# Depthwise filters of a convolution layer on sixteen 32x32 parts of TensorE, with half a block moved there from VectorE and the steps reordered

## Chip, cores and metric

The kernel runs on one core of one Trainium2 chip. The metric is the time of one execution in device microseconds (us). It is given as the median of several runs; the profile comes from one further execution with the hardware profiler on.

## What is computed

The reference chains four convolution layers over a tensor x of 32 images, 96 channels and 56 x 56 pixels in fp32. Each layer adds its result to its input, and takes as input a group normalisation of x (32 groups of three channels). The change concerns layer 0 alone, an inverted bottleneck with squeeze and excite:

```
def _L0_conv_ref(x, w_exp, ..., w_dw, ..., w_se1, b_se1, w_se2, b_se2, w_proj, ...):
    identity = x                                        # x is already group-normalised
    h = jnp.einsum('nchw,oc->nohw', x, w_exp)           # 96 -> 576 channels
    h = jax.nn.silu(_bn(h, g1, b1, m1, v1))
    h = conv_general_dilated(h, w_dw, padding='SAME', feature_group_count=MID)   # 3x3 depthwise
    h = jax.nn.silu(_bn(h, g2, b2, m2, v2))
    s = h.mean(axis=(2, 3))
    s = jax.nn.silu(s @ w_se1.T + b_se1)                # squeeze, 576 -> 24
    s = jax.nn.sigmoid(s @ w_se2.T + b_se2)             # excite, 24 -> 576
    h = h * s[:, :, None, None]
    h = jnp.einsum('nchw,oc->nohw', h, w_proj)          # project, 576 -> 96
    return _bn(h, g3, b3, m3, v3) + identity
...
x = x + _L0_conv_ref(_gn(x), ...)
```

Layers 1 to 3 (a wavelet convolution, a quantised bottleneck and a 9 x 9 diffusion filter) follow in the same program and are not touched.

## The kernel before

Layer 0 works through the 32 images one by one. The 576 inner channels make four and a half blocks of 128 partitions. The last half block holds 64 channels and is computed twice, once in each half of the partitions, which makes five blocks. An image has four tiles of 14 rows (`NP` = 4); the columns of a tile are split by parity (`j`), so that one TensorE product has 392 columns.

The work on one image is cut into steps. Each step is a letter in a hand-written order string, `L0_ORDER`, followed by up to two digits for the block and the tile or tap:

- `s`, `u`, `m`, `q`, `v`, `w`, `b`, `n`: the group normalisation. `s` and `q` are full passes on ScalarE that sum the image and its squares (L267); `u` and `v` are tiny TensorE products over the groups (L272); `m`, `w`, `b` are small VectorE steps (L276 to L290), `w` with one on GpSimd; `n` writes the normalised image `xn` (L295). `r` scales the image in place for the residual (L301).
- `e` (block, tile): expand. TensorE multiplies `xn` by the expanding weights (L309), and ScalarE evicts the result with batch norm and SiLU into a padded image `hpad` (L313).
- Blocks 0, 1 and 2 have their 3 x 3 depthwise filter on VectorE: `f` is the first tap, on ScalarE (L321), the eight `t` are the others, one `scalar_tensor_tensor` over the whole block each (L326), and `z` is the second batch norm and SiLU in place on ScalarE (L332), which also accumulates the channel sums.
- Blocks 3 and 4 (called AB and C) have their filter on TensorE, `a` and `c`: for each of nine taps four products with 64 x 64 diagonal matrices on four quarters of the array (`quarters`, L349), into one PSUM buffer, evicted by `silu2` (L332). Two of the four swap the upper and the lower 64 channels, so that all four parts of the array are in use.
- `g0` to `g4`: the channel sums are added up (VectorE), the squeeze (TensorE L379, ScalarE L381), the excite (TensorE L386), the gates (VectorE L391 and L392, ScalarE L393) and the projecting weights times the gates, `wg` (VectorE L397).
- `p` (tile): project. For each parity five products add up in PSUM, three with `h2` of blocks 0 to 2 (L407), one with `hab` (L409), one with `hc` (L410). `d` adds the result to the image on VectorE (L415).
- `o`: channel statistics for the next layer's normalisation (VectorE L88, L89), then on SP's queue the store of the image to `y0` in six DMAs (L425), the load of image b + 3 into the buffer that image b leaves (`fetch`, L196; there are three such buffers), and some seven sets of copies, here called table copies, that lay out filter tables of later layers in DRAM (L520, L547).

`run_steps` walks the order string once per slot n; a step with `+` works on image n + 1, with `-` on image n - 1. TensorE, VectorE and ScalarE run their instructions in exactly this order (`manual_schedule`), each waiting only for data and buffers; a step issues to its engines in the place where it stands. SP's queue is in order as well. PSUM has three buffers `mm` of two banks for all the large products and two small ones `sm` for the tiny products. `hpad` has two padded images that blocks 0 to 2 take in turn, and one each for AB and C; `h2` has five full-size buffers.

Of the kernel before, what the change touches and what calls it, by code (L numbers as in the profile page):

```python
# [25 lines left out]
RT = 7  # L26
# [36 lines left out]
    e00 e01 e02 e03 z0- f0 a3- z2- c1- e10 e11 t01 t02 g0- e12 t03 e30 e40 g1- s+ e13 t04 g2- g3-  # L63
    e31 e32 t05 e33 g4- t06 t07 u+ f1 m+ t11 p0- p1- q+ t08 d0- v+ w+ p2- t12 e41 d1- p3- d2- t13
    t14 e20 e21 d3- o- b+ t15 e42 t16 e43 e22 e23 f2 a0 t17 t21 a1 n+ t22 t18 t23 t24 t25 t26 t27 r
    z1 t28 c0 a2
# [9 lines left out]
class Shared:  # L76


    def load(self, nc, w):
        for t, n in ((self.grp, "group"), (self.ident, "ident"), (self.bias1, "l1_bias")):  # L80
            nc.sync.dma_start(t, w[n])
# [76 lines left out]
def window(t, p, dy, dx, r0, rows):  # L158

    at = (r0 + 1 + dy) * PITCH + 1 + dx  # L160
    return t[:p, at : at + rows * PITCH].rearrange("p (r w) -> p r w", w=PITCH)[:, :, 0:W]
# [3 lines left out]
def layer0(ctx, tc, S, x, w, y0, norm1, tables, aside):  # L165
# [8 lines left out]

    nc = tc.nc
# [3 lines left out]
    psum = ctx.enter_context(tc.tile_pool(name="l0p", bufs=3, space=PSUM))  # L179
    psm = ctx.enter_context(tc.tile_pool(name="l0q", bufs=2, space=PSUM))  # L180
    DV, AB, CC = 3, 3, 4
    ND = NBLK + 1
    COL = (0, 1, 2, 3, 5)
    HALF = 64

    def load(name, shape):
        t = cp.tile(shape, F32, tag=name, name=name)
        nc.sync.dma_start(t, w[name])
        return t
# [12 lines left out]
    wdw = load("l0_wdw", [128, ND, 9])  # L202
    wse1 = load("l0_wse1", [128, ND, SEH])
    wse2 = load("l0_wse2", [SEH, ND * 128])
    bse1 = load("l0_bse1", [SEH, 1])
    wproj = load("l0_wproj", [128, ND + 1, C])
# [25 lines left out]
    eye2 = cp.tile([128, HALF], F32, tag="eye2", name="eye2")  # L232
    diag = cp.tile([128, 2, 9, HALF], F32, tag="diag", name="diag")
# [6 lines left out]
    nc.vector.tensor_tensor(eye2, S.ident[:, :HALF], S.ident[:, HALF:], ALU.add)  # L240
    for k in (AB, CC):
        for t in range(9):
            nc.vector.tensor_scalar(diag[:, k - AB, t, :], eye2, wdw[:, COL[k], t : t + 1], None, ALU.mult)
    late = ctx.enter_context(tc.tile_pool(name="l0l", bufs=1))
    h2s += [late.tile([128, H, W], F32, tag=f"h2{i}", name=f"h2{i}") for i in (2, 3)]
    hab = late.tile([128, NP, 2, NT], F32, tag="hab", name="hab")
    wg = late.tile([128, ND + 1, C], F32, tag="wg", name="wg")
    h2s.append(late.tile([128, H, W], F32, tag="h24", name="h24"))
    hc = late.tile([128, 2, 2, NT], F32, tag="hc", name="hc")
# [3 lines left out]
    def image(b):  # L253

        if b not in ims:
            ims[b] = {
                "b": b, "xt": xs.pop(b), "h2": [None] * DV, "ps": [None] * NP,
                "pad": [hpad[(DV * b + k) % 2] for k in range(DV)] + hpad[2:],
                "ss": sm.tile([128, ND], F32, tag="ss", name="ss"),
            }  # L260
        return ims[b]
# [8 lines left out]
    def group_sum(im, name):  # L270
        im["ps" + name] = psm.tile([C, 1], F32, tag="sm", name="pn")
        nc.tensor.matmul(im["ps" + name], S.grp, im[name], start=True, stop=True)  # L272
# [46 lines left out]
    def first_tap(im, k):  # L319
        im["h2"][k] = h2s[(DV * im["b"] + k) % len(h2s)]  # L320
        nc.scalar.activation(im["h2"][k], window(im["pad"][k], 128, -1, -1, 0, H), AF.Copy,  # L321
                             scale=wdw[:, k, 0:1])

    def tap(im, k, t):
        h2 = im["h2"][k]
        nc.vector.scalar_tensor_tensor(  # L326
            h2, window(im["pad"][k], 128, t // 3 - 1, t % 3 - 1, 0, H), wdw[:, k, t : t + 1],
            h2, ALU.mult, ALU.add,
        )

    def silu2(c, view, ps, accum):
        nc.scalar.activation(view, ps, AF.Silu, bias=bi[1][:, c : c + 1], scale=sc[1][:, c : c + 1],  # L332
                             accum_out=accum)
# [4 lines left out]
    def quarters(k, pad, tiles):  # L338


        ps = psum.tile([128, 2, 512], F32, tag="mm", name="psd")
        for t in range(9):
            for j in range(2):
                for r in range(2):
                    c = r ^ j
                    p = slice(r * HALF, (r + 1) * HALF)
                    at = (2 * tiles[r] * RT + t // 3) * PITCH + t % 3
                    v = pad[p, at : at + 2 * RT * PITCH].rearrange("p (r w) -> p r w", w=PITCH)
                    nc.tensor.matmul(  # L349
                        ps[c * HALF : (c + 1) * HALF, j, :NT].rearrange("p (r w) -> p r w", w=W2),  # L350
                        diag[p, k - AB, t, :], v[:, :, j:W:2], start=(t == 0), stop=(t == 8),
                    )
        return ps

    def depthwise_ab(im, i):
        if i == 0:
            im["hab"] = hab
            im["pab"] = sm.tile([128, 2, NP], F32, tag="pab", name="pab")
        ps = quarters(AB, im["pad"][AB], (i, i))
        for j in range(2):  # L360
            silu2(3 + j, im["hab"][:, i, j, :], ps[:, j, :NT], im["pab"][:, j, i : i + 1])

    def depthwise_c(im, i):

        if i == 0:
            im["hc"] = hc
            im["pc"] = sm.tile([128, 2], F32, tag="pc", name="pc")
        ps = quarters(CC, im["pad"][CC], (2 * i, 2 * i + 1))
        silu2(5, im["hc"][:, i], ps[:, :, :NT], im["pc"][:, i : i + 1])


    def totals(im):
        nc.vector.tensor_reduce(im["ss"][:, 3:5], im["pab"], AX.X, ALU.add)
        nc.vector.tensor_tensor(im["ss"][:, 5:6], im["pc"][:, 0:1], im["pc"][:, 1:2], ALU.add)

    def squeeze(im):
        ps = psm.tile([SEH, 1], F32, tag="sm", name="pse")
        for k in range(ND):
            nc.tensor.matmul(ps, wse1[:, k, :], im["ss"][:, k : k + 1], start=(k == 0), stop=(k == ND - 1))  # L379
        im["s1g"] = sm.tile([SEH, 1], F32, tag="s1g", name="s1g")  # L380
        nc.scalar.activation(im["s1g"], ps, AF.Silu, bias=bse1, scale=1.0 / HW)  # L381

    def excite(im):
        im["pg"] = psm.tile([128, ND], F32, tag="sm", name="pg")
        for k in range(ND):
            nc.tensor.matmul(im["pg"][:, k : k + 1], wse2[:, k * 128 : (k + 1) * 128], im["s1g"],  # L386
                             start=True, stop=True)

    def gates(im):
        gt = im["gate"] = sm.tile([128, ND + 1], F32, tag="gate", name="gate")  # L390
        nc.vector.tensor_tensor(gt[:, :ND], im["pg"], mid[:, 8, :], ALU.add)  # L391
        nc.vector.tensor_tensor(gt[:, ND:], im["pg"][:, ND - 1 : ND], mid[:, 8, ND - 1 : ND], ALU.add)  # L392
        nc.scalar.activation(gt, gt, AF.Sigmoid)  # L393

    def gated(im):
        im["wg"] = wg
        nc.vector.tensor_tensor(im["wg"], wproj, im["gate"].unsqueeze(2).to_broadcast([128, ND + 1, C]),  # L397
                                ALU.mult)

    def project(im, i):  # L400
        wg = im["wg"]
        rows = slice(2 * i * RT, 2 * (i + 1) * RT)
        ps = im["ps"][i] = psum.tile([128, 2, 512], F32, tag="mm", name="psj")
        for j in range(2):
            out = ps[:C, j, :NT]
            for k in range(DV):
                nc.tensor.matmul(out.rearrange("c (r w) -> c r w", w=W2), wg[:, k, :],  # L407
                                 im["h2"][k][:, rows, j::2], start=(k == 0), stop=False)
            nc.tensor.matmul(out, wg[:, 3 + j, :], im["hab"][:, i, j, :], start=False, stop=False)  # L409
            nc.tensor.matmul(out, wg[:, 5 + (i % 2 ^ j), :], im["hc"][:, i // 2, j, :], start=False, stop=True)  # L410
# [9 lines left out]
    def store(im):  # L420
# [16 lines left out]
        "e": expand, "f": first_tap, "t": tap, "z": end_block, "a": depthwise_ab, "c": depthwise_c,  # L437
# [840 lines left out]
def layouts(a):  # L1278
# [7 lines left out]
    def quartered(v):  # L1286


        v = blocks(v)
        ba = np.concatenate([v[64:, 3], v[:64, 3]])  # L1290
        cc = np.concatenate([v[:64, 4], v[:64, 4]])
        return np.concatenate([v[:, :4], ba[:, None], cc[:, None]], axis=1)
# [7 lines left out]

    def apart(v):

        v = np.concatenate([v, v[:, -1:]], axis=1)
        v[64:, -2] = 0.0
        v[:64, -1] = 0.0
        return v

    def columns(names, blocks):
# [11 lines left out]
        "l0_wdw": quartered(a[i0 + "w_dw"].reshape(MID, 9)),  # L1320
        "l0_wse1": quartered(a[i0 + "w_se1"].T),
        "l0_wse2": quartered(a[i0 + "w_se2"]).transpose(2, 1, 0).reshape(SEH, (NBLK + 1) * 128),
        "l0_bse1": a[i0 + "b_se1"].reshape(SEH, 1),
        "l0_wproj": apart(quartered(a[i0 + "w_proj"].T)),
# [9 lines left out]
        "l2_w2": quartered(a[i2 + "w2"].reshape(MID, 9))[:, [0, 1, 2, 3, 5]],  # L1334
# [34 lines left out]
```

## Time and profile before

| | us |
|---|---|
| median of 3 runs | 6412.01 |
| lowest and highest run | 6397.1, 6412.93 |
| the profiled execution's own time | 6501.16 |
| its span, first to last instruction | 6499.3 |
| layer 0's first image statistics (L88) in it | 182.9 |
| layer 0's last image statistics in it | 3340.9 |

All durations below come from the profiled execution. Engines are PE (TensorE matmul), PEld (its weight loads), DVE (VectorE), ACT (ScalarE), POOL (GpSimd) and SP (SyncE, which issues DMAs). A line of the costliest groups reads: source line, engine, operation, out<-in by the program's names, shapes, count | busy us in all, mean ns of one | idle time of the engine just before them and what ended it. A line of a timeline reads: start, duration, engine, line, operation, names, shape, count, and in brackets the idle time before it with its releaser. A line of waits reads: who waited <- for whom: us in all, times, longest. The end of a matmul in the trace is modelled, so starts are the better measure of TensorE's pace.

### The profile page before, as it was taken

How to read it: one execution, taken by the hardware profiler on the slowest of the kernel's cores; microseconds unless marked ns; L12 is line 12 of the kernel's file. 1: busy time of each engine (PE TensorE's matmuls, PEld its weight loads, DVE VectorE, ACT ScalarE, POOL GpSimd, SP SyncE). 2: the span in 40 equal slices, each digit the busy share in tenths (PEclk: the TensorE clock that was granted, in tenths of full speed). 3: DMA queues.
4: the chain of work that ended last, by engine and by line, in shares of the span. 5: the costliest groups of instructions: out<-in, count | busy, mean ns of one | idle time of the engine just before them, and what ended most of it. 6: DMA issues, size and time to landing. Idle time of an engine off the chain costs nothing.

```text
span 6499.3 us, 115397 instructions
## 1 busy us (share of the span) xinstructions
PE 6025.5 (93%) x49064; PEld 3599.1 (55%) x49064; DVE 5168.3 (80%) x5469; ACT 3953.6 (61%) x5268; POOL 234.1 (4%) x157
## 2 busy tenths in 40 slices
PE   6989989998998998989969999989999999999699
PEld 3444444444444444444535666667777777778344
DVE  8989979898998998989957766657777767676587
ACT  6556555655656565556635565557767766677355
POOL 4000000000000000000000000000000000000000
PEclk8999999999999999989979999999999999999899
DMA  2486475839539439474655776656869695953888
GB/s 80 29 41 50 41 43 41 46 44 40 47 41 41 43 47 42 39 41 39 17 60 143 141 155 150 143 36 45 48 42 50 44 49 41 51 38 31 166 253 248
DMA packets 1631554, 452.94 MB, mean 70 GB/s; under 512 B 1447406, under 2 KB 1625318, under 8 KB 1627582
## 3 DMA queue, kind: packets, MB, share of 16 engines
q1 hardware_dynamic: 1631038, 445.55, 65.7%
q8 instruction: 386, 6.32, 0.6%
q14 instruction: 130, 1.06, 0.1%
HBM read 284.44 MB, written 214.08 MB: 77 GB/s over the span
## 4 chain that ended last, share of the span: by engine, by line
PE 71%; ACT 9%; DMA 9%; SPq 6%; DVE 3%; issue 1%; POOL 1%; ACTq 0%; DVEq 0%
PE psd L349 14%; PE psd L1019 11%; PE ps L309 9%; PE psj L407 8%; PE pc L735 6%; PE ps L1000 5%; SPq L425 4%; DMA y<-xt 4%; PE pc L1175 3%; PE psj L1056 3%; PE psj L409 3%; PE psj L410 2%; ACT hi L972 2%; ACT a L990 2%; DVE h L326 2%; PE pc L719 2%
## 5 line engine op out<-in xcount | busy, mean ns | idle before, releaser
L326 DVE SCALAR_TENSOR_TENSOR h<-hpad,l_wdw,h 128x3136 f32<-128x3136 f32 x768 | 2659.6, 3480 | 28.7 <-ACT h L321 14.9
L349 PE MATMUL psd<-hpad,diag 64*64 64x392 f32 x13824 | 1239.6, 512 | 13.4 <-issue 13.4
L313 ACT ACTIVATE hpad<-ps,o,s 128x784 f32<-128x784 f32 x640 | 684.3, 1081 | 773.3 <-PE ps L309 771.3
L309 PE MATMUL ps<-xn,l_wexp 96*128 96x392 f32 x2560 | 931.6, 516 | 135.6 <-ACT hpad L313 129.1
L1019 PE MATMUL psd<-apad,diag 64*64 64x392 bf16 x20736 | 931.5, 332 | 110.4 <-ACT a L990 57.2
L349 PEld LDWEIGHTS psd<-hpad,diag 64*64 64x64 f32 x13824 | 547.5, 132 | 694.9 <-issue 656.8
L1019 PEld LDWEIGHTS <-diag 64*64 64x64 bf16 x20736 | 695.6, 107 | 342.3 <-issue 164.7
L309 PEld LDWEIGHTS ps<-xn,l_wexp 96*128 96x128 f32 x2560 | 493.4, 197 | 524.2 <-ACT hpad L313 135.3
L565 ACT COPY T<-raw 32x112 f32<-32x112 f32 (+2 forms) x1440 | 462.8, 384 | 308.1 <-DMA raw<-tdiff 223.3
L990 ACT ACTIVATE u<-ps,o,s 128x784 int16<-128x784 f32 x576 | 536.3, 1002 | 162.0 <-PE ps L1000 143.6
L990 ACT ACTIVATE a<-psd,o,s 128x784 int16<-128x784 f32 x448 | 423.7, 999 | 327.7 <-PE psd L1019 327.7
L407 PE MATMUL psj<-h,wg 128*96 128x392 f32 x1536 | 591.4, 520 | 27.9 <-ACT hpad L313 26.4
L1000 PE MATMUL ps<-hi,l_w1q 96*128 96x392 f32 x1280 | 462.4, 361 | 10.0 <-ACT hi L972 9.2
L1175 PE MATMUL pc<-x,T 128*112 128x416 f32 (+1 forms) x1152 | 415.2, 523 | 48.1 <-DMA raw<-tdiff 47.6
L735 PE MATMUL pc<-x,T 128*112 128x416 f32 (+1 forms) x1152 | 445.8, 523 | 0.0
L1000 PE MATMUL ps<-lo,l_w1q 96*128 96x392 f32 x1280 | 438.0, 342 | 0.0
L407 PEld LDWEIGHTS psj<-h,wg 128*96 128x96 f32 x1536 | 249.4, 166 | 289.3 <-issue 258.3
L1175 PEld LDWEIGHTS pc<-x,T 128*112 128x112 f32 x1152 | 204.7, 178 | 258.1 <-issue 240.7
L332 ACT ACTIVATE hab<-psd,o,s 128x392 f32<-128x392 f32 x256 | 170.6, 671 | 263.5 <-PE psd L349 263.5
L332 ACT ACTIVATE h<-h,o,s 128x3136 f32<-128x3136 f32 x96 | 287.9, 2999 | 19.7 <-DVE h L326 19.7
L321 ACT ACTIVATE h<-hpad,l_wdw 128x3136 f32<-128x3136 f32 x96 | 279.1, 2907 | 9.3 <-DMA twav<-zwav 8.3
L735 PEld LDWEIGHTS pc<-x,T 128*112 128x112 f32 x1152 | 190.9, 178 | 143.9 <-issue 143.9
(202 smaller groups left out, 6793.5 us busy)
## 6 DMA issues: line engine op xcount, KB each, us to landing
X<-y SPq DMA_DIRECT2D x192, 392.0 KB
xt<-in_x_dram SPq DMA_DIRECT2D x32, 1176.0 KB
y<-xt SPq DMA_DIRECT2D x192, 196.0 KB
y<-y SPq DMA_DIRECT2D x96, 392.0 KB
xt<-y SPq DMA_DIRECT2D x96, 392.0 KB
out_dram<-y SPq DMA_DIRECT2D x96, 392.0 KB
y<-xt SPq DMA_DIRECT2D x90, 392.0 KB
twav<-zwav SPq DMA_DIRECT2D x768, 36.8 KB
```

The costliest lines, as they stand in the source:

```text
L309: nc.tensor.matmul(ps[:, j, :NT], wexp[:, k * 128 : k * 128 + 128], im["xn"][:, j, rows, :].rearrange("c h w -> c (h w)"), start=True, sto ...
L313: nc.scalar.activation(window(im["pad"][k], 128, 0, 0, 2 * i * RT, 2 * RT).rearrange("p r (w j) -> p j r w", j=2), ps[:, :, :NT].rearrange ...
L326: nc.vector.scalar_tensor_tensor(h2, window(im["pad"][k], 128, t // 3 - 1, t % 3 - 1, 0, H), wdw[:, k, t : t + 1], h2, ALU.mult, ALU.add,)
L332: nc.scalar.activation(view, ps, AF.Silu, bias=bi[1][:, c : c + 1], scale=sc[1][:, c : c + 1], accum_out=accum)
L349: nc.tensor.matmul(ps[c * HALF : (c + 1) * HALF, j, :NT].rearrange("p (r w) -> p r w", w=W2), diag[p, k - AB, t, :], v[:, :, j:W:2], start ...
L407: nc.tensor.matmul(out.rearrange("c (r w) -> c r w", w=W2), wg[:, k, :], im["h2"][k][:, rows, j::2], start=(k == 0), stop=False)
L565: nc.scalar.copy(to.rearrange("x t (p s) -> x t p s", p=NPH), v[:, k])
L735: nc.tensor.matmul(ps[:PH, to], st["T"][j][:, h, k, :], st["x"][:, j, h, of], start=False, stop=(n == NK - 1))
L990: nc.scalar.activation(out, ps, AF.Identity, bias=o[:, c : c + 1], scale=s[:, c : c + 1])
L1000: nc.tensor.matmul(ps[:, j, :NT], w1[:, k * 128 : k * 128 + 128], im[part][:, r0 : r0 + RT, :].rearrange("c h w -> c (h w)"), start=(part ...
L1019: nc.tensor.matmul(ps[q, j, :NT].rearrange("p (r w) -> p r w", w=W), diag[p, k, t, :], v, start=(t == 0), stop=(t == 8))
L1175: nc.tensor.matmul(ps[:, :, to], st["T"][:, h, k, :], st["x"][:, h, :, of], start=(n == 0), stop=(n == NK - 1))
```

## The change

Layer 0's filters on TensorE now use sixteen 32 x 32 parts of the array. The new `parts` replaces `quarters`. It takes two PSUM buffers (four banks) at once. For every tap it issues sixteen products with 32 x 32 diagonal matrices: shift `s` picks the column parity and the tile and owns one bank, and row part `r` writes to partition quarter `(r + s) % 4`. The channels of a shift's output are thus turned by `s` quarters, and the weights that meet them later (batch norm, squeeze, excite, project) are laid out in as many turned copies. One call covers two tiles of a block; so `a` is two calls per image in place of four, and `c` is one in place of two.

Block 2 is split. Its upper two tiles stay on VectorE (`f2`, `t2x`, `z2` on 28 rows, buffer `h2c`); its lower two go to TensorE in a new step `x0` (output `hd`). The number of columns of sums, gates and projecting weights grows: `ND` from 6 to 12, the gated weights from 7 to 14 groups. The project step still makes five products per parity: for the lower two tiles, `hd` takes the place of block 2's `h2`.

PSUM is one pool of four two-bank buffers, from which the tiny products are served too. `h2` has three full buffers and one half. The order of the steps is new: image n + 1's first block is expanded at the end of a slot; `g0` and `g1` stand at the end of the slot, `g2-` to `g4-` open the next, `p` and `d` follow in its first half, `s+` comes after `p1-`, and `x0`, `a0`, `c0`, `a1` follow one another on TensorE.

The setting up of the layer changes with it (27 small diagonal products in place of 18, and other layouts of the weights, made before the launch). The core of the diff:

```diff
-L0_ORDER: e00 e01 e02 e03 z0- f0 a3- z2- c1- e10 e11 t01 t02 g0- e12 t03 e30 e40 g1- s+ e13 t04 g2- g3-
-    e31 e32 t05 e33 g4- t06 t07 u+ f1 m+ t11 p0- p1- q+ t08 d0- v+ w+ p2- t12 e41 d1- p3- d2- t13
-    t14 e20 e21 d3- o- b+ t15 e42 t16 e43 e22 e23 f2 a0 t17 t21 a1 n+ t22 t18 t23 t24 t25 t26 t27 r
-    z1 t28 c0 a2
+L0_ORDER: g2- g3- e40 t01 g4- e12 t02 t03 e30 t04 e41 e13 p0- d0- p1- s+ u+ t05 p2- m+ r t06 d1- t07 d2-
+    p3- q+ f1 t08 e42 d3- e31 e32 e33 e20 v+ e21 o- w+ t11 e22 e23 t12 b+ e43 f2 t13 t14 t21 t15 z0
+    x0 t16 a0 t22 t17 t18 n+ c0 t23 z1 t24 t25 t26 a1 t27 e00+ t28 z2 e01+ e02+ g0 e03+ g1 f0+ e10+
+    e11+
...
-    psum = ctx.enter_context(tc.tile_pool(name="l0p", bufs=3, space=PSUM))
-    psm = ctx.enter_context(tc.tile_pool(name="l0q", bufs=2, space=PSUM))
-    DV, AB, CC = 3, 3, 4
-    ND = NBLK + 1
-    COL = (0, 1, 2, 3, 5)
+    psum = ctx.enter_context(tc.tile_pool(name="l0p", bufs=4, space=PSUM))
+    DV, XX, AB, CC = 3, 2, 3, 4
+    COL = (0, 1, 2, 6, 10)
+    ND, NW = 12, 14
+    QU = 32
...
-    for k in (AB, CC):
+    for k in (XX, AB, CC):
         for t in range(9):
-            nc.vector.tensor_scalar(diag[:, k - AB, t, :], eye2, wdw[:, COL[k], t : t + 1], None, ALU.mult)
+            nc.vector.tensor_scalar(diag[:, k - XX, t, :], eye4, wdw[:, k, t : t + 1], None, ALU.mult)
...
+                "h2": [h2s[2 * b % 3], h2s[(2 * b + 1) % 3], h2c],
...
     def group_sum(im, name):
-        im["ps" + name] = psm.tile([C, 1], F32, tag="sm", name="pn")
+        im["ps" + name] = psum.tile([128, 2, 512], F32, tag="mm", name="pn")[:C, 0, :1]
...
-    def quarters(k, pad, tiles):
-        ps = psum.tile([128, 2, 512], F32, tag="mm", name="psd")
+    def parts(im, k, tile, out, accum, col):
+        ps = [psum.tile([128, 2, 512], F32, tag="mm", name="psd") for _ in range(2)]
         for t in range(9):
-            for j in range(2):
-                for r in range(2):
+            for s in range(4):
+                for r in range(4):
+                    p, q = (slice(x % 4 * QU, (x % 4 + 1) * QU) for x in (r, r + s))
+                    at = (2 * tile(r, s) * RT + t // 3) * PITCH + t % 3
+                    v = im["pad"][k][p, at : at + 2 * RT * PITCH].rearrange("p (r w) -> p r w", w=PITCH)
                     nc.tensor.matmul(
+                        ps[s // 2][q, s % 2, :NT].rearrange("p (r w) -> p r w", w=W2),
+                        diag[p, k - XX, t, :], v[:, :, s % 2 : W : 2], start=(t == 0), stop=(t == 8),
                     )
+        for s in range(4):
+            silu2(col(s), out[s], ps[s // 2][:, s % 2, :NT], accum(s))
+    def depthwise_ab(im, g):
+        parts(im, AB, lambda r, s: 2 * g + s // 2, [hab[:, 2 * g + s // 2, s % 2] for s in range(4)],
+              lambda s: im["pq"][:, g, s : s + 1], lambda s: COL[AB] + s)
+    def depthwise_c(im, _):
+        parts(im, CC, lambda r, s: 2 * (r // 2) + s // 2, [hc[:, s] for s in range(4)],
+              lambda s: im["pc"][:, s : s + 1], lambda s: COL[CC] + s % 2)
+    def depthwise_x(im, _):
+        parts(im, XX, lambda r, s: 2 + s // 2, [hd[:, s] for s in range(4)],
+              lambda s: im["ss"][:, XX + s : XX + s + 1] if s else im["px"], lambda s: XX + s)
...
     def project(im, i):
...
-            for k in range(DV):
+            s = 2 * (i % 2) + j
+            for k in range(DV if i < 2 else XX):
                 nc.tensor.matmul(out.rearrange("c (r w) -> c r w", w=W2), wg[:, k, :],
                                  im["h2"][k][:, rows, j::2], start=(k == 0), stop=False)
-            nc.tensor.matmul(out, wg[:, 3 + j, :], im["hab"][:, i, j, :], start=False, stop=False)
-            nc.tensor.matmul(out, wg[:, 5 + (i % 2 ^ j), :], im["hc"][:, i // 2, j, :], start=False, stop=True)
+            if i >= 2:
+                nc.tensor.matmul(out, wg[:, XX + s, :], hd[:, s], start=False, stop=False)
+            nc.tensor.matmul(out, wg[:, COL[AB] + s, :], hab[:, i, j], start=False, stop=False)
+            nc.tensor.matmul(out, wg[:, COL[CC] + (s + i // 2 * 2) % 4, :], hc[:, s], start=False, stop=True)
```

The excite step makes twelve products with windows of the weights (`wse2`) in place of six; the squeeze runs over `ND` columns as before.

## The prediction

> **What bounds the kernel now.** I read the page's costliest groups first: layer 0 owns the longest VectorE group (L326, the filter taps) and the longest TensorE groups.
>
> ```profile
> span 6499.3 us, 115397 instructions
> ...
> L326 DVE SCALAR_TENSOR_TENSOR h<-hpad,l_wdw,h 128x3136 f32<-128x3136 f32 x768 | 2659.6, 3480 | 28.7 <-ACT h L321 14.9
> L349 PE MATMUL psd<-hpad,diag 64*64 64x392 f32 x13824 | 1239.6, 512 | 13.4 <-issue 13.4
> ...
> L349 PEld LDWEIGHTS psd<-hpad,diag 64*64 64x64 f32 x13824 | 547.5, 132 | 694.9 <-issue 656.8
> ```
>
> Then busy time by stretch, each from one image's statistics (first step of the store) to the next's. Columns: length, busy PE, weight loads, DVE, ACT, POOL, granted clock, DMA.
>
> ```profile
> 1111.80:1229.40 117.60, 101.96 (x621) 51.23 (x620) 92.94 (x53) 62.06 (x62) 3.63 (x1) 0.91 1.11 39
> 1229.40:1325.70 96.30, 94.89 (x621) 46.47 (x620) 92.67 (x52) 62.01 (x62) 3.63 (x1) 1.00 0.59 47
> 1518.50:1639.80 121.30, 98.64 (x621) 48.76 (x620) 92.75 (x52) 62.14 (x62) 3.63 (x1) 0.89 1.33 36
> ```
>
> An undisturbed image takes 96.3 us with PE busy 95 and DVE 93: both are full, PE a little more. Some images take 20 to 25 us more with no more work. The waits and the queue's timeline say why:
>
> ```profile
> ACT junk L267 <- DMA xt<-in_x_dram: 138.6, 7, 27.0
> ...
> 1600.08 2.82 ACT L267 ACTIVATE junk<-xt 96x3136 bf16<-96x3136 f32 x1 [22.92 <-DMA xt<-in_x_dram]
> ```
> ```profile
> 1422.31 27.64 SPq L425 DMA_DIRECT2D y<-xt  x6
> ...
> 1460.23 0.34 SPq L196 DMA_DIRECT2D xt<-in_x_dram  x1
> ...
> 1518.64 53.45 SPq L425 DMA_DIRECT2D y<-xt  x6
> ...
> 1592.60 0.32 SPq L196 DMA_DIRECT2D xt<-in_x_dram  x1
> ```
>
> The store of image b frees the buffer into which image b+3 is loaded. It usually takes 38 us (1422.3 to 1460.2), but 74 us in every third to fifth image. From the statistics of b to the first sum (L267) of b+3 the order leaves 58.5 us; a slow store needs 74 + 7.5 for the load = 81.5. So seven images stall by some 23 us. First to last statistics are 182.9 to 3340.9: 31 images at 101.9 on average.
>
> PE's pieces, from its timeline:
>
> ```profile
> 1517.21 8.06 PE L309 MATMUL ps<-xn,l_wexp 96*128 96x392 f32 x24
> 1525.21 25.59 PE L349 MATMUL psd<-hpad,diag 64*64 64x392 f32 x288
> 1550.73 5.53 PE L309 MATMUL ps<-xn,l_wexp 96*128 96x392 f32 x16
> ...
> 1575.85 0.46 PE L379 MATMUL pse<-ss,l_wse 128*24 128x1 f32 x12
> ...
> 1577.75 1.49 PE L386 MATMUL pg<-s1g,l_wse 24*128 24x1 f32 x12
> ```
>
> Each fp32 product is two records. An expand step of four records takes 1.32 us, so one product alone 0.656. The 288 records of L349 are 36 taps of four products on four 64x64 parts: 0.711 us a tap, so four run in almost the time of one.
>
> **What the Trainium skill says.** "TensorE: Matmul & The Clock Gate", Part 3 (Packing small matmuls): sixteen 32x32 tiles run at once, measured 10.6 times faster than in turn. The trace has no 32x32 part; its four 64x64 parts agree in kind. Part 1 (The HAM clock gate) of that page: after an idle window of about 3.4 us PE runs at half clock until one such window is busy; the stalled stretches agree (0.89 and 0.91 granted, against 1.00). "TensorEngine Tiling (Array Packing)", Gotcha 1: different row tiles may not write one PSUM bank at once. The new code sends the four row parts of a shift to four partition quarters, and each shift to its own bank, so this needs no waiting.
>
> **The change, part by part, for one undisturbed image.**
>
> *DVE.* Of 24 taps, 16 stay at 3.476 us (48.66/14). Eight halve: 1568 of 3136 elements; at 392 elements L415 takes 0.616, so about 1.04 ns an element plus 0.21, hence 1.84. Saved: 8 x 1.64 = 13.1. The gated weights grow from 672 to 1344 columns (0.85 to 1.55), totals by 0.1. 92.7 - 13.1 + 0.8 = 80.4.
>
> *PE.* Expand 20 x 1.32 = 26.4 and project 4 x 6.78 = 27.1 stay: it still makes ten products per step. Filters: 54 taps of four products become 36 taps of sixteen, two calls for AB, one each for C and half of block 2. With X us a tap: 36X for 38.5. Squeeze and excite double from 12 to 24 records: 0.81 + 2.95 us. Small ones 0.2. Sum 57.5 + 36X.
>
> *X* is not in the trace. Bounds: 0.656 (perfect); 0.894 if the 0.06 us that a tap loses today with eight load-multiply pairs grows with 32 pairs. I take 0.80: 57.5 + 28.8 = 86.3. Worse values are rivals.
>
> *ACT.* L321 and L332 on block 2 halve (-3.0), eight more accumulating evictions of 392 columns at 0.72 start to start replace two of 784: about +3.7. Near 63: not a bound.
>
> *The new order.* The sums give 86; the order gives more, which I get by walking the queues. Time 0 is t01.
> - DVE: t01, g4, t02 to t04 to 15.5; d0 (p0 ends 13.2), t05, m (u after p1, 20.1), t06, d1, t07, d2, t08 to 33.1. d3 waits 0.8 for p3 (33.7). Statistics 35.0 to 39.2; w waits 1.3 for v, which stands behind five expands. t11 needs first tap f1, which waits on ACT for p3 (it reuses that buffer) and ends at 36.8: in time. Then 8 full and 8 half taps without a wait to 83.
> - The end of the slot is exposed. Before, t01 and t02 covered the last SiLU, and later taps most of the squeeze, excite and gate (DVE waited 0.63 us for L386). Now g0 follows t28 and needs z2 on ACT: 2.0 idle. After g0 DVE has only g3's additions, and t01 is behind them. PE squeezes (0.8), ACT finishes three expand evictions before s1g, PE does e10 and e11 (2.6) and excites (2.95): 6.5 idle.
> - Idle 0.8 + 1.3 + 2.0 + 6.5 = 10.6, so 80.4 + 10.6 = 91. PE itself then idles some 6 us ahead of the squeeze; if its clock falls, e10, e11 and the excite lose 0 to 4 us. I take 2: **93 us**, against 96.3.
> - PSUM: four two-bank buffers serve all, and one filter call takes two. x0 to a1 run back to back, each waiting for evictions of the call two before (2.9 us against 9X = 7): covered. If not, each call shows it as an ACT wait.
> - X is hidden as long as a1's eviction, then e00's, finish before t28: a1 must end by 79.7, it starts its chain at 45.5, so 36X up to 34.2, **X up to 0.95**. Above, each 0.1 costs 3.6 us.
>
> *Moved steps and SP.* Only the store step issues DMAs: six stores, the fetch, then seven sets of table copies. SP is occupied 77 us for a usual image and 113 for a slow one; at 93 the following store starts late, but its fetch still lands in time. Statistics to the first sum is now 58 + 7.4 = 65.4; before DVE needs m there are 9 us more, 75 in all. Behind a late first sum on ACT stand the residual, the second sum, f1 and the evictions; m holds DVE. A slow store stalls 81.5 - 75 = 6.5, with aftermath 8, where it was 25: 7 x 8 = 56.
>
> *Ends.* Until the first statistics DVE has eight half taps fewer and the expands start earlier: 15 us less, between 5 and 25. The set-up has 27 small diagonal products for 18, at half size: nothing, beside DMA.
>
> *Sum.* 31 x 93 + 56 = 2939 for 3158, less 15: -234. The profiled execution takes 6501.2 (span 6499.3), 1.4% over the median 6412.0; scaled, -231. **6180 us.**
>
> **Rivals.**
> 1. *The sixteen parts do not stream together* (eight at a time, or SBUF feeding four streams per partition at half rate): X = 1.42. For: each partition now feeds four products where it feeds two, and a tap already takes 8% more than one product. Against: four parts cost only that 8%. Image: 93 + 36 x 0.47 = 110, stalls gone: 31 x 110 - 15 - 3158 = +237: 6645. The sign turns where 31 images equal 3173, at 102 us: X = 1.21.
> 2. *Weight loads run in turn.* L386 gives (1.49-0.25)/11 = 0.113 us for 128 columns, L379 (0.46-0.16)/11 = 0.027 for 24: 0.034 for 32. 32 loads: X = 1.08. Against: the page's loads are busy 547.5 us for 13824, 40 ns each, while one takes 132, so they overlap. Image 97.7, stalls 4: -140 or so: 6270.
> 3. *The exposed slot end is covered after all*, and the sums rule: 86.3 an image. A shorter image leaves the slow store less cover, 13 us each: 31 x 86.3 + 91 - 15 - 3158 = -407: 6010. Against: t01 follows the gate on DVE.
> 4. *A wash*: unprofiled, stores could be shorter, so that fewer stalls vanish, and the clock costs more: 6400.
>
> **Numbers.** Forecast 0.65; rival 1 0.15, rival 2 0.12, rival 3 0.05, wash 0.03. The forecast's own range is 6090 (slot end 3 us shorter) to 6290 (no stalls to save: 31 x 3.3 + 15 = 117, and 2 us of clock kept). Rival 2 lies inside; leaving out rivals 1 and 3 and part of the wash, the range is 6070 to 6310. About 0.3% (19 us) is what a measurement of this kernel tells from no change. Faster 0.82, same 0.03, slower 0.15.
>
> **What would show it.** L326 in two shapes, 3.48 and about 1.84 us, 512 and 256 of them. Matmuls of 32*32, 36864 records, busy 800 to 1030 us in all (36X x 32). Undisturbed stretches of 91 to 95 with DVE busy near 80 and PE's share below 95. DVE idle before the gate additions, about 6 us an image, released by L386's successor. Waits for the loaded image falling from 138.6 to below 90, and now m on DVE in their wake. It is wrong if a tap of sixteen takes over 0.95, if the gate wait is below 2 us, or if layers 1 to 3 (3341 to 6499) move by more than 20 us.

## The result, and the profile after

The changed kernel takes **6741.65 us** (median of four runs, 6720.57 to 6752.97) against 6411.14 before: 1.0517 times as long, with a 95% interval from 1.0486 to 1.0548. The prediction said 6180.

The head of the page after and its costliest groups:

```profile
span 6751.2 us, 163645 instructions
...
L328 DVE SCALAR_TENSOR_TENSOR h<-hpad,l_wdw,h 128x3136 f32<-128x3136 f32 x512 | 1780.6, 3478 | 6.9
L350 PE MATMUL psd<-hpad,diag 32*32 32x392 f32 x36864 | 1276.7, 567 | 354.6 <-issue 352.6
L350 PEld LDWEIGHTS psd<-hpad,diag 32*32 32x32 f32 x36864 | 758.4, 108 | 866.9 <-issue 672.4
...
L328 DVE SCALAR_TENSOR_TENSOR h2c<-hpad,l_wdw,h2c 128x1568 f32<-128x1568 f32 x256 | 473.5, 1850 | 5.7
```

VectorE is relieved as foretold: 512 full and 256 half taps of 3.478 and 1.850 us. The news is at the end of the L350 line. The filters' products were preceded by 354.6 us in which PE stood still, and 352.6 of that is "issue": PE waited for nothing that the profile shows. Before, the same column read 13.4.

Layer 0 runs from 168.1 (first image statistics) to 3607.1 (last): 110.9 us an image, for 101.9 before. What follows layer 0 takes 3144 us for 3158, so the whole loss lies in it. Two stretches from one image's statistics to the next (length, busy PE, weight loads, DVE, ACT, POOL, granted clock, DMA share, GB/s):

```profile
1957.00:2060.10 103.10, 94.82 (x1365) 55.41 (x1364) 80.42 (x54) 61.64 (x74) 3.63 (x1) 0.97 0.24 43
2162.70:2291.50 128.80, 105.26 (x1365) 58.24 (x1364) 80.46 (x53) 62.28 (x74) 3.63 (x1) 0.87 0.91 34
```

Same instructions, DVE at the predicted 80.4 in both, and 26 us between them. Both have a store; in the longer one it is a slow one, and the DMA engines are busier (0.91 against 0.24). PE's and SP's timelines show how the slow store and the filters meet:

```profile
2173.53 4.74 PE L350 MATMUL psd<-hpad,diag 32*32 32x392 f32 x157
2179.07 1.15 PE L350 MATMUL psd<-hpad,diag 32*32 32x392 f32 x27 [0.80 <-issue]
2185.97 5.84 PE L350 MATMUL psd<-hpad,diag 32*32 32x392 f32 x128 [5.74 <-issue]
2195.47 6.15 PE L350 MATMUL psd<-hpad,diag 32*32 32x392 f32 x128 [3.66 <-issue]
2205.25 5.10 PE L350 MATMUL psd<-hpad,diag 32*32 32x392 f32 x128 [3.62 <-issue]
2216.39 5.97 PE L350 MATMUL psd<-hpad,diag 32*32 32x392 f32 x127 [6.05 <-issue]
```
```profile
2162.83 45.23 SPq L432 DMA_DIRECT2D y<-xt  x6
...
2225.10 0.34 SPq L196 DMA_DIRECT2D xt<-in_x_dram  x1
```

From the second pause on, PE stops after every 128 matmul records (one less is a record missing from the trace). With the weight loads that is 256 records, a fixed block. These pauses fall between the issue of the image's store (2162.8) and its end, which lets the load of another image go (2225.1). A block resumes only every 9.5 to 11 us, though 128 records are four taps and take 3.7 us. Beside a usual store, as in the shorter stretch, the blocks resume 5 to 6 us apart:

```profile
1976.11 3.93 PE L350 MATMUL psd<-hpad,diag 32*32 32x392 f32 x128 [1.18 <-issue]
1982.33 5.24 PE L350 MATMUL psd<-hpad,diag 32*32 32x392 f32 x128 [2.29 <-issue]
1987.72 3.92 PE L350 MATMUL psd<-hpad,diag 32*32 32x392 f32 x127 [0.16 <-issue]
1992.79 3.91 PE L350 MATMUL psd<-hpad,diag 32*32 32x392 f32 x128 [1.15 <-issue]
```

Over the whole layer, blocks between two pauses take 4.2 to 7.0 us beside usual stores (median 5.4, 39 blocks) and 6.4 to 11.6 beside slow ones (median 9.8, 21 blocks). Of the 352.6 us, 242 fall into a store and 82 into the 12 us after it, while the next image is loaded.

So the first suspicion: **PE runs out of instructions.** The queues table has a line for them, first before, then after.

```profile
q8 instruction: 386, 6.32, 0.6%
```
```profile
q8 instruction: 572, 9.37, 0.7%
```

The change adds 163645 - 115397 = 48248 instructions and 186 packets of this queue: 259 instructions a packet, and 9.37 MB / 572 = 16.4 KB each. The Trainium skill describes this in "Runtime: NRT & Kernel Launch", Instruction fetch mechanics: an engine's instructions come in blocks of 16 KiB, 256 instructions, over a DMA queue of its own. The block's size agrees with the trace. The page adds that this fetching is hidden, because issuing an instruction takes longer than fetching one; the pauses above contradict that here.

The trace keeps the packets of this queue too. In the slow store above, four of them land at 2184.3, 2193.8, 2203.1 and 2213.7, and PE goes on 1.7, 1.7, 2.2 and 2.7 us later: each pause ends when a block of instructions has come. Each packet took only 1.7 to 2.6 us; from the landing of one to the start of the next 6.8 to 8.9 us passed. Over the layer, 128 of the 149 pauses longer than 0.5 us end 1.2 to 3.2 us after such a landing; of the filter products at large 39% start that long after one.

This also fits the kernel before, which hardly showed it. Its 288 matmul records of L349 were 36 taps at 0.711 us, so a block of 128 lasted 11.4 us, about the longest of the intervals beside a slow store. Now a block lasts 3.7 us, less than the 4.2 to 7.0 us beside a usual one.

### The profile page after: what moved, and what is told of

Same layout as the page of the kernel before. It is cut to its first block, busy times and chain, and to the rows that moved or that the text cites. A ratio compares the mean times of both kernels' runs of the same rounds, so it can differ in the third digit from the quotient of the medians.

```text
span 6751.2 us, 163645 instructions
## 1 busy us (share of the span) xinstructions
PE 6111.6 (91%) x72872; PEld 3872.3 (57%) x72872; DVE 4771.4 (71%) x5510; ACT 3954.2 (59%) x5652; POOL 228.9 (3%) x157
## 2 busy tenths in 40 slices
DMA packets 1631743, 456.46 MB, mean 68 GB/s; under 512 B 1447406, under 2 KB 1625318, under 8 KB 1627582
## 3 DMA queue, kind: packets, MB, share of 16 engines
q8 instruction: 572, 9.37, 0.7%
## 4 chain that ended last, share of the span: by engine, by line
PE 84%; issue 6%; ACT 6%; DVE 1%; DMA 1%; SPq 1%; POOL 0%; ACTq 0%; DVEq 0%
PE psd L350 19%; PE ps L311 13%; PE psd L1026 10%; PE psj L412 7%; PE pc L1182 6%; PE pc L742 6%; PE ps L1007 6%; PE psj L1063 3%; PE psj L416 2%; PE psj L417 2%; ACT hi L979 2%; PE pc L726 2%; ACT a L997 2%; PE pg L394 1%; PE pa L700 1%
## 5 line engine op out<-in xcount | busy, mean ns | idle before, releaser
L328 DVE SCALAR_TENSOR_TENSOR h<-hpad,l_wdw,h 128x3136 f32<-128x3136 f32 x512 | 1780.6, 3478 | 6.9
L350 PE MATMUL psd<-hpad,diag 32*32 32x392 f32 x36864 | 1276.7, 567 | 354.6 <-issue 352.6
L350 PEld LDWEIGHTS psd<-hpad,diag 32*32 32x32 f32 x36864 | 758.4, 108 | 866.9 <-issue 672.4
L311 PE MATMUL ps<-xn,l_wexp 96*128 96x392 f32 x2560 | 947.6, 527 | 21.4 <-DVE nm L278 12.6
L311 PEld LDWEIGHTS ps<-xn,l_wexp 96*128 96x128 f32 x2560 | 507.4, 202 | 402.8 <-issue 88.8
L328 DVE SCALAR_TENSOR_TENSOR h2c<-hpad,l_wdw,h2c 128x1568 f32<-128x1568 f32 x256 | 473.5, 1850 | 5.7
L412 PE MATMUL psj<-h,wg 128*96 128x392 f32 x1024 | 397.9, 509 | 2.3 <-DVE wg L403 2.3
L323 ACT ACTIVATE h<-hpad,l_wdw 128x3136 f32<-128x3136 f32 x64 | 186.2, 2910 | 247.7 <-PE psj L412 247.7
```

Source lines behind the costliest of these rows:

```text
L311: nc.tensor.matmul(ps[:, j, :NT], wexp[:, k * 128 : k * 128 + 128], im["xn"][:, j, rows, :].rearrange("c h w -> c (h w)"), start=True, sto ...
L328: nc.vector.scalar_tensor_tensor(h2, window(im["pad"][k], 128, t // 3 - 1, t % 3 - 1, 0, h2.shape[1]), wdw[:, k, t : t + 1], h2, ALU.mult, ...
L350: nc.tensor.matmul(ps[s // 2][q, s % 2, :NT].rearrange("p (r w) -> p r w", w=W2), diag[p, k - XX, t, :], v[:, :, s % 2 : W : 2], start=(t ...
```

## The experiments

F below stands for this theory, that the fetch of instructions beside the store starves PE. Against it stand S, that the sixteen products are slow themselves in streaming their columns, and L, that their weight loads run in turn. The expectations call the runs e1 to e12; each heading names its own. Their totals for the pauses, 466 and 592 us, are larger than the 352.6 us that stand before the matmuls on the page. Ratios are to the kernel before as it was measured beside each run (6385.5 to 6392.7 us).

**The store in long runs (e1, e2).** The image is stored in pieces of 56 bytes (one row of a parity). This run writes the same bytes as one run per channel, at other places of `y0`:

```diff
-            for to, of in groups(xt, y0, lambda y: y[:, :, b, :], store=True):
+            for to, of in groups(xt, y0, lambda y: in_runs(y)[:, b], store=True):
```

It was done to the kernel after and to the kernel before.

> The kernel after, but layer 0's store writes each channel's image as one long run (12.5 KB) in place of 224 runs of 56 B: the same bytes, at other places of the scratch tensor, so that later layers read permuted data. Theory F (TensorE runs out of instructions: its records are fetched in blocks of 256, which wait behind the store's small packets): the pauses of 1 to 6 us between blocks (466 us in all in layer 0) go, a filter call falls from 12.9 to about 8.5 us, an image from 104-109 (127 with a slow store) to 93-96, and the whole to 6741 - 31 x 15 = about 6250 to 6300. Theory S (sixteen streams cannot be fed) and theory L (weight loads in turn): a filter call stays at 12 to 13 us; only what a slow store costs beside it may go, at most 8 x 20 = 160, so 6580 or more.

> The kernel before with the same long runs in layer 0's store. Both theories: the seven stalls of 23 to 26 us go, since the store no longer holds back the load of the image after next; an image takes 96.3 throughout: 6411 - 180 = about 6230. If the 64x64 filters, with 38 percent of the records per image, had been short of instructions too, an image falls below 96.

After with long runs: **6239.66 us**, 0.9768 (0.9739 to 0.9796) of before's 6388.8. This is 10 us below the range of theory F. The layer's instructions on TensorE, VectorE and ScalarE are untouched, yet the pauses are gone:

```profile
L354 PE MATMUL psd<-hpad,diag 32*32 32x392 f32 x36864 | 1088.1, 522 | 30.1 <-issue 27.6
```
```profile
1601.84 28.55 PE L354 MATMUL psd<-hpad,diag 32*32 32x392 f32 x968
1630.76 5.63 PE L354 MATMUL psd<-hpad,diag 32*32 32x392 f32 x184 [0.38 <-issue]
```

The image's four calls (1152 records) run through with one gap of 0.38 us here. Layer 0 runs from 167.6 to 3100.2, 94.6 us an image. The sums agree: from after to this kernel the L350 group loses 1276.7 - 1088.1 = 189 us of busy time (its ends are modelled and stretch over pauses) and 325 us of "issue", together 514; layer 0's first-to-last statistics lose 3439 - 2933 = 506, and the medians 502.

Before with long runs: 6300.52, 0.9863 (0.9833 to 0.9893), where 6230 had been expected: a miss. Its images take 96.3 us throughout, as the undisturbed ones did. But the stalls behind slow stores were worth only 6388.8 - 6300.5 = 88 us in ordinary runs, not the 173 (3158 - 31 x 96.3) of the profiled execution, which was some 90 us longer than the ordinary runs of the same kernel; stalls that were longer in it fit that difference. Its slow stores took 69 to 78 us; in the profile of the order "between" further down, with the same stores, they take 59 to 61.

**Fewer columns, fewer weights (e3, e4).** In the kernel after, taps 1 to 8 leave out half of their 392 columns, or half of the 32 output channels.

```diff
-    ps[s // 2][q, s % 2, :NT], ... v[:, :, s % 2 : W : 2]
+    ps[s // 2][q, s % 2, : NT // (2 if t else 1)], ... v[:, : 2 * RT // (2 if t else 1), s % 2 : W : 2]
```
```diff
-    ps[s // 2][q, ...], diag[p, k - XX, t, :]
+    ps[s // 2][q.start : q.start + QU // (2 if t else 1), ...], diag[p, k - XX, t, : QU // (2 if t else 1)]
```

> The kernel after with taps 1 to 8 of TensorE's filters on 196 of 392 columns each: the same records, half the columns streamed (part of the filter left out). Theory S: a tap falls from 0.93 to about 0.5 us, a call from 12.9 to about 7, the whole to about 6350. Theories F and L: tap and call stay within 10 percent (0.85 to 0.95; 12 to 13 us), the whole within 60 us of 6741.

> The kernel after with taps 1 to 8 of TensorE's filters on 16 of the 32 weight columns (32 rows x 16 columns; part of the filter left out): the same records and the same streams, weight loads half as long. Theory L: a tap falls from 0.93 towards 0.71, and a call by 2 us. Theories F and S: no change beyond 3 percent in the tap, the call or the whole (6741).

Half the columns took 6677.28 us, half the weights 6693.66, one run each: 1.045 and 1.048 times the 6388.8 of the kernel before, where the kernel after has 1.052.

```profile
L350 PE MATMUL psd<-hpad,diag 32*32 32x196 f32 (+1 forms) x36864 | 999.8, 434 | 547.0 <-issue 543.5
```
```profile
L350 PE MATMUL psd<-hpad,diag 32*16 32x392 f32 (+1 forms) x36864 | 1230.9, 554 | 339.3 <-issue 338.0
```

With almost half of the streaming gone, the time falls by 1%. The products are busy 277 us less, and 191 of these reappear as pauses (352.6 to 543.5). That is what a supply limit does: PE finishes each block sooner and waits longer for the next. The expectation under F was wrong in one point: a tap of half the columns without a pause does fall, to 0.62 us in the median, as S had it; but the call and the whole hardly follow, and the whole is 64 us below 6741 where F allowed 60. Narrower weights change hardly anything; a tap without a pause, start to start, has a median of 0.90 us for 0.92, so weight loads in turn (rival 2) are not it.

**Fewer records (e5).** Taps 1 to 8 keep two of four row parts, 80 products a call in place of 144:

```diff
-                for r in range(4):
+                for r in range(2 if t else 4):
```

> The kernel after with taps 1 to 8 of TensorE's filters on half of the sixteen products (row parts 0 and 1 alone; part of the filter left out): 80 products a call for 144, each with full columns and weights. Theory F (instructions run out): 1280 filter records per image for 2304, so the pauses fall by more than half, from 592 us and less to below 200, a call to 8 us or less, and the whole to 6230 to 6330. Theory S (streams): each part still streams as long as before, two row parts leave half of the load on SBUF; a tap falls too, but the pauses between blocks of records have no reason to go.

6395.18 us, one run: 346 us off, more than five times what half the columns brought, and the pauses fall to 69.3. In kind this is F's answer. In size it is a miss: an image still takes 99.5 us on average (93 to 112). Most of the pauses left, some 52 us, stand in images with a slow store; with 69.3 us in all they do not account for the whole of the miss, and the rest stays open.

```profile
L350 PE MATMUL psd<-hpad,diag 32*32 32x392 f32 x20480 | 970.2, 554 | 70.0 <-issue 69.3
```

**The reverse, in the kernel before (e6).** Each of its filter products becomes two of 196 columns: the same columns and results, twice the records.

```diff
-        for t in range(9):
+        for n, t in ((n, t) for n in range(2) for t in range(9)):
...
-    ps[c * HALF : (c + 1) * HALF, j, :NT], ... v[:, :, j:W:2]
+    ps[c * HALF : (c + 1) * HALF, j, n * NT // 2 : (n + 1) * NT // 2], ... v[:, n * RT : (n + 1) * RT, j:W:2]
```

> The kernel before with every filter product on TensorE in two of 196 columns: the same sums on the same 64x64 parts, 1728 filter records per image for 864. Theory F: pauses of 1 us and more appear in L349's stream where the store runs, where before has none, though fewer than after, since a block of 256 records lasts 5.7 us for 3.9; an image takes 3 to 15 us more, the whole 6480 to 6850. Theory S: the columns streamed are the same, so no pauses; only 1 to 3 us an image for the more records, under 6500.

6484.35 us for 6391.3, one run. The time lies at the edge between the two expectations and decides nothing. The trace does: the pattern appears in a kernel that did not have it, 121.8 us of "issue" for 13.4, here beside a slow store issued at 1513.1. A block now lasts 5.7 us, about what a usual store lets through, and 117 of the 121.8 us stand in images with a slow store.

```profile
1519.67 8.71 PE L349 MATMUL psd<-hpad,diag 64*64 64x196 f32 x187
1536.77 7.15 PE L349 MATMUL psd<-hpad,diag 64*64 64x196 f32 x128 [8.38 <-issue]
1546.28 7.46 PE L349 MATMUL psd<-hpad,diag 64*64 64x196 f32 x128 [2.35 <-issue]
1555.10 5.93 PE L349 MATMUL psd<-hpad,diag 64*64 64x196 f32 x128 [1.36 <-issue]
```

**Long runs and half the columns together (e8)**, to see the pace of sixteen parts without small packets.

> The long runs of e1 with the half columns of e3 (part of the filter left out), to read the pace of a tap without pauses. If the columns set it (0.90 in e1), it falls to 0.5; if the 32 load and multiply pairs do, it stays at 0.85 to 0.90. The time moves little either way, since the end of the slot and VectorE set an image: 6200 to 6240.

6263.2 us, one run, 23 us above the range. A tap without a pause falls from 0.90 to 0.56 in the median, so with long runs the 0.90 is set by the columns: sixteen parts together take 1.38 times as long as one product alone (0.656), and no fixed cost per product holds them there. But pauses come back, 303.2 us:

```profile
1614.78 2.47 PE L354 MATMUL psd<-hpad,diag 32*32 32x196 f32 x128 [0.66 <-issue]
1618.53 2.84 PE L354 MATMUL psd<-hpad,diag 32*32 32x196 f32 x127 [1.27 <-issue]
1621.84 2.87 PE L354 MATMUL psd<-hpad,diag 32*32 32x392 f32 x128 [0.47 <-issue]
1625.96 2.45 PE L354 MATMUL psd<-hpad,diag 32*32 32x196 f32 x128 [1.25 <-issue]
```

From start to start these blocks are 3.7, 3.3 and 4.1 us apart. So even without the store's small packets PE is supplied with about 256 records each 3.7 us, and four full taps at 0.90 use just that. In this run 230 of the 234 pauses over 0.5 us end 1.2 to 1.7 us after a packet of the instruction queue has landed; of the filter products at large 18% start that long after one. The changed kernel runs at the edge of its supply, and the store pushes it over.

**The other order alone (e7, e9, e10).** A part of the change's plan was to begin the sums of the next image later, so that a slow store no longer stalls them. In the kernel before, with its filters as they were, this was tried three times (only moved steps shown):

```
# s, u, m, q, v, w in before: e40 g1- s+ e13 ... t07 u+ f1 m+ t11 p0- p1- q+ t08 d0- v+ w+ p2- t12
# late:    ... e41 s+ d1- p3- u+ d2- t13 m+ q+ t14 e20 e21 v+ d3- w+ o- ...
# later:   ... e41 s+ d1- p3- u+ d2- t13 t14 e20 e21 d3- m+ q+ o- t15 e42 v+ w+ t16 e43 b+ ...
# between: ... g4- t06 s+ t07 f1 t11 p0- u+ p1- t08 m+ d0- q+ p2- v+ t12 e41 d1- p3- d2- w+ ...
```

> The kernel before with the first sum, its group mean and what follows them about seven taps later in the order (s after e41, u after p3, m and q after t13, v after e21, w after d3), nothing else. From the statistics of image b to the first sum of b + 3 it leaves some 83 us for 58.5, a slow store with the load needs 81.5: the seven stalls of 23 to 26 us go, images take 96 to 97 throughout, and the whole falls by 150 to 180 to 6210 to 6260. If the stalls were something else than that wait, they stay: 6390.

> The kernel before with the first sum as late as in e7, but m and q after d3, and v and w after the last expand of block C's third tile, so that VectorE does not wait 3.6 us an image at m for the group mean that stands behind p3 on TensorE. No stall and images of 96.3 to 97: the long runs of e2 gave the kernel before 6300 in ordinary runs, so 6290 to 6330. If the 98.8 us an image of e7 came from somewhere else than this wait: 6370 to 6390 again.

> The kernel before with the first sum three taps later only (s after t06, u between p0 and p1, m after t08, v after p2, w after d2): some 10 to 12 us more for a slow store. The profile of before has stalls of 25 us, seven of them, but its ordinary runs lie only 91 us above those with long runs (e2), 13 us a stall. If ordinary stalls are 13 us, this takes nearly all of them: 6300 to 6340. If they are as long as in the profile, less than half: 6350 or more, and stalls of 10 to 15 us stay in this profile.

Late: 6378.81, ratio 0.9982 (0.9973 to 0.999), a miss. The stalls are gone, but every image pays for it: `m` waits 3.6 us for the sum that TensorE makes behind the projects, so images take 98.8.

```profile
DVE nm L276 <- PE pn L272: 105.2, 29, 3.6
```

Later: 6497.81, ratio 1.0163 (1.0144 to 1.0182), a miss on the other side. TensorE now reaches `v` before ScalarE has finished `q`, and VectorE runs ahead of a first tap:

```profile
DVE h L326 <- ACT h L321: 121.8, 60, 7.8
...
PE pn L272 <- ACT junk L267: 101.6, 30, 23.2
```

Between: **6287.39, ratio 0.9837** (0.9819 to 0.9855), images at 95.4, and of the wait for the loaded image (138.6 us before) 8.3 us are left. This is 13 us below the range expected. So this part of the change was worth having by itself.

**The store away from the filters, in the kernel after (e11, e12).** The last two runs leave the sixteen-part filters and the 56-byte runs as they are, and move the store behind `a1`, so that it falls beside the expands, whose 4 records take 1.32 us. The next image's sums and normalisation move too, since the image's buffer comes free later. `y` stands for the six stores, the fetch and the table copies, taken out of `o`:

```diff
+    ... z0 x0 s+ t16 a0 u+ t22 m+ q+ t17 c0 v+ t18 w+ t23 z1 t24 b+ n+ t25 t26 a1 y- t27 e00+ ...
```

> The kernel after with its short-run store as it is, but issued after a1, the last filter step of a slot, instead of after d3, ahead of the filters; so that the next image is there later, s, u, m, q, v, w, b and n move behind x0. Theory F: a usual store (38 us) is over before the next filters, only a slow one reaches into them; the pauses fall from 355 us to below 150, images take 95 to 99, those behind a slow store 10 to 20 more, and the whole 6270 to 6400. If the pauses do not come from the store beside the filters, they stay, and the time with them: 6700.

6719.29, ratio 1.0527 (1.05 to 1.0553): no change, and a miss. The step moved in the order, but the transfer did not: the order binds TensorE, VectorE and ScalarE, and SP issues the store as soon as its image is ready, still ahead of the filters.

```profile
1503.31 26.86 SPq L435 DMA_DIRECT2D y<-xt  x6
```
```profile
1513.81 7.39 PE L350 MATMUL psd<-hpad,diag 32*32 32x392 f32 x245
1522.73 3.92 PE L350 MATMUL psd<-hpad,diag 32*32 32x392 f32 x128 [1.52 <-issue]
```

So the store was given something to wait for: ScalarE copies one column of the image onto itself at this place.

```diff
+        nc.scalar.copy(xt[:, 0, 0:1], xt[:, 0, 0:1])
         if b < B - 1:
             for to, of in groups(xt, y0, lambda y: y[:, :, b, :], store=True):
```

> e11 with the store really held back. In e11 it stood after a1 in the order but started with the filters as in after, since SP waits only for d3; here a copy of one column of the stored image onto itself, on ACT behind a1's evictions, is what the store waits for. Theory F: a usual store is over before the next filters and a slow one reaches only into the first; pauses fall from 305 us to below 150, a filter call from 12 to 9.5 us or less, an image to 96 to 100, behind a slow store 10 to 20 more; the whole 6300 to 6420. If the pauses have nothing to do with the store running beside the filters, it stays at 6700 or goes above.

**6279.30 us, ratio 0.9829** (0.9806 to 0.9853), 440 us below the run before it. Products, columns and packets are those of the kernel after, and the order is that of the run before it; beside the one copy only the store's moment differs.

```profile
L350 PE MATMUL psd<-hpad,diag 32*32 32x392 f32 x36864 | 1107.9, 525 | 26.7 <-issue 18.0
```
```profile
1562.11 5.53 PE L311 MATMUL ps<-xn,l_wexp 96*128 96x392 f32 x16
...
1623.20 16.39 PE L350 MATMUL psd<-hpad,diag 32*32 32x392 f32 x576
```
```profile
1570.76 28.08 SPq L436 DMA_DIRECT2D y<-xt  x6
...
1607.77 0.34 SPq L196 DMA_DIRECT2D xt<-in_x_dram  x1
```

The store now runs after one image's filters (over at 1562) and before the next image's (from 1623). "Issue" falls from 298.0 to 18.0 us, a filter call of nine taps takes (1107.9 + 26.7) / 128 = 8.9 us on average for 12.7 in the kernel after, and images take 95.2; the whole is 21 us below the range expected. This shows the cause with nothing left out of the computation: the filters starve where the store with its small packets runs beside them, and hardly where it does not.

## Why the prediction was wrong

Most of its steps came out, which the run with long runs shows best, since hardly anything disturbs it.

- **DVE**, 80.4 an image: 80.42 after; half taps 1.850 for 1.84.
- **The order.** 93 us an image: 94.6 with long runs. The walk through the queues named most of the waits; VectorE's waits in that run, over 31 images (us in all, times, longest):

```profile
DVE gate L402 <- PE pg L398: 209.4, 31, 10.3
DVE ss L382 <- ACT h2c L338: 81.8, 31, 4.3
DVE xt L426 <- PE psj L421: 69.9, 46, 8.5
DVE nm L282 <- PE pn L278: 49.7, 29, 2.3
DVE ve L286 <- PE pn L278: 39.6, 29, 1.4
```

  An image waits 6.8 us for the gate where 6.5 were forecast, 2.6 for z2 (2.0), 2.3 at the `d` steps (0.8), 1.3 at w (1.3), and 1.6 at m, which was to wait for nothing. Together they are 14.5, where the prediction had 10.6 and 2 for the clock; the difference is about the 1.6 us by which its image was too short. Rival 3, a covered slot end, is refuted by the 6.8.
- **The head**, 15 us: first statistics at 168.1 for 182.9. Layers 1 to 3 moved by 14 us.
- **X**, the pace of a tap, taken at 0.80 between 0.656 and 0.894: 0.90 to 0.92 in the median where no pause falls into it. That is just above the upper bound, but under the 0.95 up to which it is hidden. With long runs the filters of an image take (1088.1 + 30.1) / 32 = 34.9 us, at the edge of the 34.2 that were to be hidden.
- **The step that failed** is the term 36X, and with it "X is hidden". It priced only the time that PE needs for its products, 28.8 us an image, and assumed that the instructions are there. After, an image's filters take 36 taps in (1276.7 + 354.6) / 32 = 51 us, which is an effective X of 1.42, and the slot ends when they do. With that X the prediction's own sum gives 110 us an image, and 110.9 were measured: the rest of the path held. The sentence "Only the store step issues DMAs" left out a second user of the DMA engines: PE itself, whose fetches had grown from one block each 11.4 us to one each 3.7. The prediction counted that 32 load-multiply pairs replace eight per tap, and used it for PE's pace alone.
- **The stalls.** They were to shrink to 56 us, from 173 in the profiled execution. The waits for the loaded image are gone after, so in kind this is right, but ordinary runs had only 88 us to give back. Between the two long-run kernels, where there are no stalls, the change brings 6300.5 - 6239.7 = 61 us; the prediction's terms for that case, 31 x 3.3 + 15, gave 117, and the 1.6 us by which an image was too short, times 31, are most of the difference.
- **The banks.** The prediction concluded from its passage on PSUM banks that nothing has to wait. Its reason does not bear that out: the four row parts of a shift do write one bank at the same time, at different partitions. The conclusion came out all the same. Had the four taken turns, a tap would take about 4 x 0.656 = 2.6 us (an estimate from the single product); it takes 0.90.

Rival 1 came nearest with 6645 and an X of 1.42. It was right in size for a reason that the runs refute: the sixteen parts do stream together, at 0.90, and halving what they stream leaves the time almost where it was.

What stays open is why a block comes so late beside the store. It is not the transfer alone: in the kernel after, a packet of the instruction queue takes 1.3 us in the median and 4.0 at most within a store, and 1.1 outside. Most of the time passes before the packet starts: ahead of the pauses over 0.5 us, 5.9 us in the median from the landing of one packet to the start of the next. That it waits behind the store's 56-byte packets fits the long-run kernel, which has 1631743 - 946975 = 684768 fewer packets for the same bytes, but no run shows that wait itself. Why every third to fifth store is slow is not shown either.

## What to carry to other kernels

When work on TensorE is cut into smaller products, count records as well as products: 256 of them are a block that has to be fetched. In this kernel PE stopped when a block was used up in less than some 3.7 us, in less than some 5.4 beside a usual store in tiny packets, or in less than some 10 beside a slow one. "Idle <-issue" in steps of 128 matmul records is the mark of it. Longer runs in the store cure it, and so does keeping the transfer and the dense stretch apart, which takes a data dependence where an order written by hand does not bind the queue. With the results unchanged, the two versions that clearly beat both kernels are the changed filters with the store held back (6279.3 us) and the old filters with the sums begun a little later (6287.4 us).

## What was not expected of the hardware

- The supply of instructions limits TensorE: about 256 records each 3.7 us without the store's small packets; beside a store in 56-byte pieces each 5.4 us in the median when the store is a usual one, and each 9.8 when it is slow.
- Sixteen 32x32 parts with 392 fp32 columns take 0.90 us a tap in the median, 1.38 times one product; so they do the work of 16 / 1.38 = 11.6 products in turn. "TensorE: Matmul & The Clock Gate", Part 3 (Packing small matmuls) of the Trainium skill has 10.6, which is of the same size, as long as the instructions arrive.
- With 196 columns a tap of 64 records takes 0.56 us, so a load-multiply pair needs no more than 0.56 / 32 us, some 17 ns.
